# A fused two-layer kernel: 1/sqrt(v) from Ln and Exp, and token normalizations moved from VectorE to ScalarE

## The chip, the core and the metric

One Trainium2 chip, of which the kernel uses one core. The metric is the device time of one execution in microseconds; a kernel's time is the median of its runs. The engines are named as in the profile: PE (TensorE matmul), PEld (its weight loads), DVE (VectorE), ACT (ScalarE), POOL (GpSimd) and SP (the engine that issues most DMAs). They run side by side, each through its own instructions in a fixed order, and wait for each other by semaphores.

## What is computed

The input is a feature map of 4 images, 384 channels, 32 x 32 pixels (1024 tokens per image), all in float32. Two layers follow each other, each with a mixing part and a part on single tokens:

```python
x = x + _L0_conv_ref(_ln_c(x), ...)     # selective scan in 4 directions, layernorm, exact gelu
t = _to_tokens(x)
t = t + _L0_ffn_ref(_ln_t(t), ...)      # mixture of 4 experts, the best 2 per token, 384 -> 1536 -> 384
x = _from_tokens(t, x)
x = x + _L1_conv_ref(_ln_c(x), ...)     # attention, 8 heads of 64, queries = keys = values
t = _to_tokens(x)
t = t + _L1_ffn_ref(_ln_t(t), ...)      # two factorized layers with a gelu between
x = _from_tokens(t, x)
```

Every `_ln` subtracts the mean over the 384 channels of a token and divides by `sqrt(variance + eps)`. These square roots, and the subtract-and-scale behind some of them, are what the change touches. The scan's own step is `h = h * exp(dt * A) + dt * u * B`, with 16 states per channel.

## The kernel before

**The scan layer** (`scan_layer`, L192 on) goes through 32 units: 4 images, 4 directions, 2 halves of 512 positions. Each unit has 3 blocks of 128 channels, and each block 4 groups of states. In a group (`chunk`, L389 on) ACT computes `da` = Exp (L429) into one of two PSUM buffers, POOL multiplies `bx` (L420), DVE runs the recurrence over 512 positions (L434), DVE (L441) or POOL (L448) multiplies with C, and PE sums over states (L455). `project` (L293 on) prepares the next unit's `dt` meanwhile, with an Abs, Relu, Exp and Ln on ACT.

**The tail** of an image is the expert layer, the attention and the last token layer. It is written behind the scan of the next image, so that PE's work for one image lies beside the scan of the next; the last image's tail stands alone at the end. The steps that matter here:

- `spread` (L606, the router) transposes token tiles, takes their statistics on DVE (L633, L634), takes the root (L636, L637), scales the gate scores (L638), and in `places` (L666) works out with some fifty small DVE instructions which row of a gathered list each token goes to (`g_pos`, L778). It reloads the tokens (`xt`, L648), normalizes each tile of 128 tokens (128x384, L649, eight per image), and POOL scatters the tile's rows to two places each (L654).
- `experts` (L807) runs 11 slots of up to 256 gathered rows through one expert's two matrices. ACT does the Gelu (L888).
- `combine` (L904) loads the tokens (`xt`), gathers each token's two results into tiles `got` (POOL, L913; 128 x 2 x 384, tag `kw`), scales them on ACT (L920) and adds them on DVE (L924). It stores `xt` (L925).
- `prologue` (L930) takes statistics (`stats`, L516: L523, L524, then L525 and L526), normalizes in place in `xt` (`normalize`, L529: L531, eight per image), and PE transposes the tiles (L939) into `xc` for the attention. Writing in place, L531 has to wait until the store L925 has read `xt`.
- `last_layers` (L1049) uses `stats` as well; its `rstd` enters at L1102.

**The root** was taken in three steps: a Sqrt on ACT, a reciprocal on DVE, and a reload of the table set that has Exp and Ln, since Sqrt stands in another set. `exp_again` (L141) issues that reload just behind the Sqrt, with priority. A Gelu has the same pattern. In `layernorm` (L150), which normalizes over channels with PE's column sums, the root is L178 and the reciprocal L180, for each half of 512 positions: 4 halves per image, two before the scan and two behind it, 16 in all.

**The order of the work** isn't written by hand. A planner simulates the engines and orders each engine's instructions by that and by priorities; the router, `combine`, `prologue` and `last_layers` are pulled forward by a priority offset (`FORWARD`). A changed instruction can therefore move others, far from it, on all engines. Tiles rotate through a fixed number of buffers per tag (`kw` 8 or 10, `k12` 2 or 3, `k4` 5 or 4); a new tile waits until the one whose place it takes has been read for the last time.

`second_layer_exact` runs only when a sum in the attention grows past a limit, which doesn't happen with these inputs.

Of the kernel before, what the change touches and what calls it, by code (L numbers as in the profile page):

```python
# [11 lines left out]
AF = mybir.ActivationFunctionType  # L12
ALU = mybir.AluOpType
# [4 lines left out]
P = 128  # L18
B = 4
D = 384  # L20
# [28 lines left out]
MB = L // P  # L49
# [65 lines left out]
class Body:  # L115
# [25 lines left out]
    def exp_again(self, ins):  # L141

        with self.tc.issue_after(ins), self.tc.high_priority():
            self.nc.scalar.preload_act_table_set("natural_log_exp_and_others")

    def col(self, name, i):
        at = COL[name][0] + i
        return self.cols[:, at : at + 1]

    def layernorm(self, src, dst, eps, psum, work):  # L150

        nc = self.nc
        for i in range(NH):
            sl = halves(i)
            mean = psum.tile([P, HF], F32, tag="ps", name="ln_mean")
            for c in range(DC):
                nc.tensor.matmul(mean, self.ones, src[:, c, sl], start=(c == 0), stop=(c == DC - 1))
            for c in range(DC):
                nc.vector.scalar_tensor_tensor(
                    dst[:, c, sl], mean, -1.0 / D, src[:, c, sl], op0=ALU.mult, op1=ALU.add  # L160
                )

            sqs = []
            for c in range(DC):
                sq = work.tile([P, HF], F32, tag="k2", name="ln_sq", bufs=6)
                nc.scalar.activation(sq, dst[:, c, sl], AF.Square)
                sqs.append(sq)
            nm = HF // P
            var = psum.tile([P, HF], F32, tag="ps", name="ln_var")
            for m in range(nm):  # L170
                for c in range(DC):
                    nc.tensor.matmul(
                        var[:, m : m + 1], sqs[c][:, m * P : (m + 1) * P], self.ones[:, :1],
                        start=(c == 0), stop=(c == DC - 1),
                    )
            std = work.tile([P, nm], F32, tag="ln_std", name="ln_std", bufs=2)
            self.exp_again(
                nc.scalar.activation(std, var[:, :nm], AF.Sqrt, bias=eps, scale=1.0 / D).ins  # L178
            )
            nc.vector.reciprocal(std, std)  # L180
            rows = psum.tile([P, HF], F32, tag="ps", name="ln_rows")
            for m in range(nm):
                nc.tensor.matmul(
                    rows[:, m * P : (m + 1) * P], std[:, m : m + 1].to_broadcast([P, P]),
                    self.ident, start=True, stop=True,
                )
            for c in range(DC):
                nc.vector.tensor_mul(dst[:, c, sl], dst[:, c, sl], rows)
# [296 lines left out]
    def first_layer(self, b, room):  # L485

        self.experts(b, self.slots, room)
        with self.tc.high_priority(offset=FORWARD):
            xt = self.combine(b, *self.place, room)
            return self.prologue(xt, xt, room)  # L490

    def second_layer(self, b, xc, room, between):
        att = self.attention(xc, self.sums[:, b], room)
# [22 lines left out]
    def stats(self, xt, eps, room):  # L516

        nc = self.nc
        st = room.tile([P, MB, 6], "st", "st")
        mv = room.tile([P, MB, 2], "mv", "mv")  # L520
        rstd = room.tile([P, MB], "rstd", "rstd")
        for m in range(MB):
            nc.vector.bn_stats(st[:, m, :], xt[:, m, :])  # L523
            nc.vector.bn_aggr(mv[:, m, :], st[:, m, :])  # L524
        self.exp_again(nc.scalar.activation(rstd, mv[:, :, 1], AF.Sqrt, bias=eps).ins)  # L525
        nc.vector.reciprocal(rstd, rstd)  # L526
        return mv[:, :, 0], rstd

    def normalize(self, xt, mean, rstd, out):  # L529
        for m in range(MB):  # L530
            self.nc.vector.tensor_scalar(  # L531
                out[:, m, :], xt[:, m, :], mean[:, m : m + 1], rstd[:, m : m + 1],
                op0=ALU.subtract, op1=ALU.mult,
            )

# [68 lines left out]
    def spread(self, b, x1, room):  # L606


        nc = self.nc
        src = x1[b].rearrange("(c p) l -> p c l", p=P)  # L610
        st = room.tile([P, MB, 6], "r_st", "st")
        mv = room.tile([P, MB, 2], "r_mv", "mv")
        rstd = room.tile([P, MB], "r_rstd", "rstd")
        sc = room.tile([P, MB, NE], "sc", "sc")


        for m in range(0, MB, 2):
            x = room.tile([P, DC, 2 * P], "k4", "x")
            nc.sync.dma_start(out=x, in_=src[:, :, m * P : (m + 2) * P])
            xt = room.tile([P, 2, D], "k4", "xt")  # L620
            for o in range(2):
                ps = room.bank("p", "tt_ps")
                cols = slice(o * P, (o + 1) * P)
                for c in range(DC):
                    nc.tensor.transpose(ps[:, c * P : (c + 1) * P], x[:, c, cols], self.ident)
                for c in range(DC):
                    nc.tensor.matmul(
                        ps[:, D : D + NE], x[:, c, cols], self.wg[:, c, :],
                        start=(c == 0), stop=(c == DC - 1),
                    )  # L630
                nc.scalar.copy(xt[:, o, :], ps[:, :D])
                nc.vector.tensor_copy(sc[:, m + o, :], ps[:, D : D + NE])
                nc.vector.bn_stats(st[:, m + o, :], xt[:, o, :])  # L633
                nc.vector.bn_aggr(mv[:, m + o, :], st[:, m + o, :])  # L634
            nc.sync.dma_start(out=self.tokens(b)[:, m : m + 2, :], in_=xt)
        self.exp_again(nc.scalar.activation(rstd, mv[:, :, 1], AF.Sqrt, bias=self.eps5).ins)  # L636
        nc.vector.reciprocal(rstd, rstd)  # L637
        nc.vector.tensor_mul(sc, sc, rstd.unsqueeze(2).to_broadcast([P, MB, NE]))  # L638
        nc.vector.tensor_add(sc, sc, self.bg.unsqueeze(1).to_broadcast([P, MB, NE]))
        pos, gate, expert = self.places(sc, room)  # L640

        placed = []
        for m in range(MB):
            if m % 2 == 0:
                xt = room.tile([P, 2, D], "k4", "xt")
                nc.sync.dma_start(out=xt, in_=self.tokens(b)[:, m : m + 2, :])  # L648
            nc.vector.tensor_scalar(  # L649
                xt[:, m % 2, :], xt[:, m % 2, :], mv[:, m, :1], rstd[:, m : m + 1],  # L650
                op0=ALU.subtract, op1=ALU.mult,
            )
            for k in range(TOP):
                put = nc.gpsimd.indirect_dma_start(  # L654
                    out=self.rows[b][:, :],
                    out_offset=bass.IndirectOffsetOnAxis(ap=pos[:, k, m : m + 1], axis=0),
                    in_=xt[:, m % 2, :], in_offset=None,
                ).ins
                for other in placed:
                    self.tc.declare_no_dep(put, other, reason="rows of different tokens")  # L660
                for other in self.zeroed:
                    self.depend(put, other)
                placed.append(put)
        return (pos, gate), (expert, placed)
# [238 lines left out]

    def combine(self, b, pos, gate, room):  # L904

        nc = self.nc
        xt = room.tile([P, MB, D], "k12", "xt")
        nc.sync.dma_start(out=xt, in_=self.tokens(b))
        got = []
        for m in range(MB):  # L910
            got.append(room.tile([P, TOP, D], "kw", "got"))
            for k in range(TOP):
                nc.gpsimd.indirect_dma_start(  # L913
                    out=got[m][:, k, :], out_offset=None, in_=self.made[b][:, :],
# [8 lines left out]
            for k in range(TOP):  # L923
                nc.vector.tensor_add(xt[:, m, :], xt[:, m, :], ps[:, k, :D])  # L924
        nc.sync.dma_start(out=self.tokens(b), in_=xt)  # L925
        return xt

    def prologue(self, xt, xn, room):  # L930

        nc = self.nc
        mean, rstd = self.stats(xt, self.eps6, room)
        self.normalize(xt, mean, rstd, xn)
        xc = room.tile([P, DC, L], "k12", "xc")
        for c in range(DC):
            ps = room.two("tc_ps")
            for m in range(MB):
                nc.tensor.transpose(  # L939
                    ps[:, m // 4, m % 4 * P : (m % 4 + 1) * P], xn[:, m, c * P : (c + 1) * P],  # L940
                    self.ident,
                )
            nc.scalar.copy(xc[:, c, :], ps.rearrange("p o l -> p (o l)"))
        return xc
# [213 lines left out]
    def second_layer_exact(self):  # L1158

        nc, tc, a = self.nc, self.tc, self.a  # L1160
        with ExitStack() as ctx:
# [10 lines left out]
            for b in range(B):  # L1172
                xc = work.tile([P, DC, L], F32, tag="xc", name="xc", bufs=1)
                att = work.tile([P, HEADS // 2, L], F32, tag="att", name="att", bufs=1)
                with ExitStack() as part:
                    room = Room(tc, part, f"e{b}", EXACT)
                    room.open_banks(part, NARROW_BANKS)
                    xt = room.tile([P, MB, D], "k12", "xt")
                    nc.sync.dma_start(out=xt, in_=self.tokens(b))
                    nc.vector.tensor_copy(xc, self.prologue(xt, xt, room))  # L1180
                with ExitStack() as part:
                    psum = part.enter_context(tc.tile_pool(name=f"e{b}_a", bufs=2, space=PSUM))
                    self.attention_exact(xc, att, work, psum)
# [202 lines left out]
```

## Time and profile before

| | |
|---|---|
| time, median of 3 runs | 4483.56 us (4473.93 to 4485.39) |
| the profiled execution, its own time | 4517.48 us |
| its span, first to last instruction | 4513.6 us |
| mean granted TensorE clock | 0.831 |
| PE, DVE, ACT, POOL busy | 3440.6, 3010.8, 2534.3, 3037.0 us |
| ACT_TABLE_LOAD, all lines | 185 of 1283 ns each |
| - of these at the Sqrt lines L178, L525, L636 | 16 + 8 + 4 |
| - of these by `exp_again` (L144) | 92: 28 behind a Sqrt, 64 behind a Gelu |
| Sqrt | 263 ns (128x4), 301 ns (128x8) |
| reciprocals of the roots on DVE | 28, 171 to 192 ns in the mean |
| normalization of a tile, DVE, L649 and L531 | 64; median 474 and 472 ns, longest 2542 and 8690 ns |

How to read it: a line of the groups gives line, engine, operation, output and inputs, shape, count, then the busy time in us and the mean in ns of one, and after the second bar the engine's idle time just before these instructions with what ended it. A line of the time line gives the start and the length in us, engine, line and count of instructions that follow one another, and in brackets the idle time before. A line of the waits gives who waited for whom, the sum in us, how often, and the longest.

The scan stage ends near 3555 us. The first 650 us hold only the scan of the first image; from then on tail and scan lie side by side; from 3555 us to the end there is only the tail. The router's normalizations run at 849, 1883, 2983 and 3640 us, those of the prologue at 1444, 2574, 3608 and 4238 us.

### The profile page before, as it was taken

The page shows a single profiled execution, that of the slowest core. Times are in us where ns is not written, and L with a number is a line of the kernel's source. Part 1 is how long each engine was busy: PE and PEld are TensorE (multiplying, and loading weights), DVE is VectorE, ACT ScalarE, POOL GpSimd, SP SyncE. Part 2 cuts the span into 40 slices and gives each one's busy share as a digit, 9 for nine tenths or more (in the row PEclk, how much of TensorE's full clock was granted, in tenths as well). Part 3 has the DMA queues.
Part 4 walks back from the last instruction along what each step waited for, and adds up shares of the span by engine and source line. Part 5 has one row for each costly group of instructions (what it writes and reads, how often), then busy time and mean ns, then how long its engine had stood idle before and what let it go on. Part 6 is the DMA issues. An engine that isn't in the chain of part 4 may idle for free. (4 is left out here: it accounts for less than half of the span.)

```text
span 4513.6 us, 46925 instructions
## 1 busy us (share of the span) xinstructions
PE 3440.6 (76%) x13852; PEld 1652.0 (37%) x13852; DVE 3010.8 (67%) x4344; ACT 2534.3 (56%) x4406; POOL 3037.0 (67%) x1467
## 2 busy tenths in 40 slices
PE   6545554479894787669998588757998689999796
PEld 2111121145552222225555222214555445556333
DVE  4999997878878977977877777896778520002102
ACT  4555554456665676466666577556666444334554
POOL 4999998788987877778988778878889510000100
PEclk7666665589996898669998699858999789999897
DMA  4444554477886533457779443445787543344200
GB/s 119 118 123 118 146 136 106 137 230 209 231 240 181 149 84 104 130 159 226 210 220 275 137 114 101 115 139 170 232 244 232 169 157 115 107 127 153 75 16 15
DMA packets 404361, 684.81 MB, mean 152 GB/s; under 512 B 50944, under 2 KB 206464, under 8 KB 404096
## 3 DMA queue, kind: packets, MB, share of 16 engines
q1 hardware_dynamic: 395360, 656.16, 50.3%
q0 software_dynamic: 8192, 25.17, 1.7%
q8 instruction: 111, 1.82, 0.2%
q14 instruction: 154, 1.26, 0.1%
q10 hardware_dynamic: 544, 0.40, 0.0%
HBM read 561.47 MB, written 120.06 MB: 151 GB/s over the span
## 5 line engine op out<-in xcount | busy, mean ns | idle before, releaser
L420 POOL TENSOR_TENSOR bx<-dtr,bcs 128x1024 f32<-128x1024 f32 x768 | 1797.8, 2366 | 227.7 <-PE acc L455 103.5
L429 ACT ACTIVATE da<-dtr,nega 128x512 f32<-128x512 f32 x1536 | 1045.5, 691 | 1039.4 <-DVE bx L441 569.0
L448 POOL TENSOR_TENSOR bx<-bx,bcs 128x1024 f32<-128x1024 f32 x384 | 903.6, 2358 | 211.8 <-DVE bx L434 88.0
L455 PE MATMUL acc<-bx,sel 128*32 128x512 f32 x3072 | 511.8, 713 | 312.4 <-POOL bx L448 248.8
L879 PE MATMUL h_ps<-xc,w 128*128 128x256 f32 (+1 forms) x3168 | 680.1, 370 | 61.7 <-DVE xc L861 31.5
L895 PE MATMUL y_ps<-w,hs 128*128 128x384 f32 x1824 | 649.9, 509 | 49.8 <-ACT hs L888 44.1
L879 PEld LDWEIGHTS h_ps<-xc,w 128*128 128x128 f32 x3168 | 557.2, 200 | 253.4 <-issue 120.4
L434 DVE TENSOR_TENSOR_SCAN bx<-da,carry,bx 128x512 f32<-128x512 f32 x384 | 474.0, 1269 | 118.6 <-POOL bx L420 65.5
L434 DVE TENSOR_TENSOR_SCAN bx<-da,bx 128x512 f32<-128x512 f32 x384 | 452.2, 1209 | 129.2 <-POOL bx L420 70.3
L434 DVE TENSOR_TENSOR_SCAN da<-da,carry,bx 128x512 f32<-128x512 f32 x384 | 476.5, 1273 | 67.9 <-ACT da L429 62.6
L441 DVE TENSOR_TENSOR bx<-da,bcs 128x512 f32<-128x512 f32 x768 | 509.8, 679 | 3.8
L434 DVE TENSOR_TENSOR_SCAN da<-da,bx 128x512 f32<-128x512 f32 x384 | 456.3, 1218 | 60.7 <-ACT da L429 44.2
L895 PEld LDWEIGHTS y_ps<-w,hs 128*128 128x128 f32 x1824 | 352.3, 198 | 341.7 <-issue 86.4
L992 ACT ACTIVATE ex<-s_ps 128x512 f32<-128x512 f32 x512 | 299.4, 591 | 274.9 <-PE s_ps L987 259.9
L987 PE MATMUL s_ps<-w 64*128 64x512 f32 x1024 | 308.4, 674 | 83.1 <-ACT ex L992 74.2
L1077 POOL TENSOR_TENSOR xt<-xt,wb 128x3072 f32<-128x3072 f32 x4 | 26.8, 6708 | 477.5 <-DMA w<-in_w 345.5
L1036 PE MATMUL o_acc<-ex,vt 128*64 128x512 f32 x1024 | 295.6, 658 | 0.8 <-ACT att L1044 0.8
L455 PEld LDWEIGHTS acc<-bx,sel 128*32 128x32 f32 x3072 | 77.7, 117 | 596.0 <-POOL bx L448 363.8
L884 ACT ACTIVATE hs<-h_ps,bb 128x256 f32<-128x256 f32 (+1 forms) x528 | 194.0, 447 | 128.8 <-PE h_ps L879 128.5
L899 DVE TENSOR_TENSOR y<-y_ps,bb 128x384 f32<-128x384 f32 x76 | 41.6, 548 | 237.6 <-PE y_ps L895 237.6
L913 POOL DMA_INDIRECT got<-made,g_pos x64 | 60.8, 950 | 192.4 <-PE f_acc L1136 159.1
L987 PEld LDWEIGHTS s_ps<-w 64*128 64x128 f32 x1024 | 81.1, 192 | 266.8 <-ACT ex L992 149.1
(216 smaller groups left out, 4021.9 us busy)
## 6 DMA issues: line engine op xcount, KB each, us to landing
w<-in_w SPq DMA_DIRECT2D x352, 576.0 KB
dtr<-dd SPq DMA_DIRECT2D x1536, 128.0 KB
bcs<-rows SPq DMA_DIRECT2D x512, 128.0 KB
dd<-one_e SPq DMA_DIRECT2D x96, 256.0 KB
dd<-mag SPq DMA_DIRECT2D x96, 256.0 KB
rows<-zero SPq DMA_DIRECT2D x76, 192.0 KB
xs<-rows SPq DMA_DIRECT2D x32, 384.0 KB
made<-y SPq DMA_DIRECT2D x32, 384.0 KB
```

The source lines that it names most:

```text
L420: pool = nc.gpsimd.tensor_mul(bx, dtr[q][1], bc[:, 0].unsqueeze(1).to_broadcast([P, 2, HF])).ins
L429: nc.scalar.activation(da, dtr[q][0][:, j, :], AF.Exp, scale=nega[:, col : col + 1])
L434: nc.vector.tensor_tensor_scan(run(h), run(da), run(bx[:, j, :]), 0.0 if first else hold, ALU.mult, ALU.add,)
L441: dve = nc.vector.tensor_mul(bx[:, j, :], h, cg).ins
L448: pool = nc.gpsimd.tensor_mul(bx, bx, cg.unsqueeze(1).to_broadcast([P, 2, HF])).ins
L455: nc.tensor.matmul(acc[lo : lo + DB, :], sel, out[q][:, j, :], start=(g == 0), stop=(g == NG - 1),)
L879: nc.tensor.matmul(ps[:, r, :], w1[(f + r) // wf][:, c, (f + r) % wf * P : ((f + r) % wf + 1) * P], xc[:, c, :], start=(c == 0), stop=(c = ...
L884: nc.scalar.activation(hs[:, f + r, :], ps[:, r, :], AF.Identity, bias=bb[:, f + r : f + r + 1])
L895: nc.tensor.matmul(out[:, :D], hs[:, f, t * P : (t + 1) * P], w2[f // wf][:, f % wf, :], start=(f == 0), stop=(f == FC - 1),)
L987: nc.tensor.matmul(ps[:, o, :], w[rows, j * P : (j + 1) * P], w[rows, halves(i)], start=True, stop=True,)
L992: ins = nc.scalar.activation(ex[:, o, :], ps[:, o, :], AF.Exp, scale=HD**-0.5, accum_out=sums[:, t, 2 * j + o, i : i + 1],).ins
L1036: ins = nc.tensor.matmul(out[cols, :], made[t][1][:, j, cols], ex[:, o, :], start=(j == 0), stop=(j == MB - 1),).ins
```

## The change

The root becomes two instructions of ACT, `Ln(scale * v + eps)` and `Exp(-0.5 * that)`, both of the set that the scan uses, so that the Sqrt, its table load, the reload and the reciprocal all go. A normalization `(x - mean) * rstd` becomes an ACT Identity with a scale `rstd` and a bias `less = -mean * rstd`, which a new DVE instruction makes once per image and site (128x8). In the prologue its output is no longer `xt` itself but the first half of the tile `got` of the same tokens, which `combine` now returns as well.

```diff
+    def inverse_root(self, out, var, eps, scale=1.0):
+
+        self.nc.scalar.activation(out, var, AF.Ln, bias=eps, scale=scale)
+        self.nc.scalar.activation(out, out, AF.Exp, scale=-0.5)
...
             std = work.tile([P, nm], F32, tag="ln_std", name="ln_std", bufs=2)
-            self.exp_again(
-                nc.scalar.activation(std, var[:, :nm], AF.Sqrt, bias=eps, scale=1.0 / D).ins
-            )
-            nc.vector.reciprocal(std, std)
+            self.inverse_root(std, var[:, :nm], eps, scale=1.0 / D)
...
-            xt = self.combine(b, *self.place, room)
-            return self.prologue(xt, xt, room)
+            xt, xn = self.combine(b, *self.place, room)
+            return self.prologue(xt, xn, room)
...
-        self.exp_again(nc.scalar.activation(rstd, mv[:, :, 1], AF.Sqrt, bias=eps).ins)
-        nc.vector.reciprocal(rstd, rstd)
+        self.inverse_root(rstd, mv[:, :, 1], eps)
         return mv[:, :, 0], rstd
 
-    def normalize(self, xt, mean, rstd, out):
-        for m in range(MB):
-            self.nc.vector.tensor_scalar(
-                out[:, m, :], xt[:, m, :], mean[:, m : m + 1], rstd[:, m : m + 1],
-                op0=ALU.subtract, op1=ALU.mult,
-            )
+    def less_mean(self, mean, rstd, room, tag):
+
+        less = room.tile([P, MB], tag, "less")
+        self.nc.vector.scalar_tensor_tensor(less, mean, -1.0, rstd, op0=ALU.mult, op1=ALU.mult)
+        return less
...
-        self.exp_again(nc.scalar.activation(rstd, mv[:, :, 1], AF.Sqrt, bias=self.eps5).ins)
-        nc.vector.reciprocal(rstd, rstd)
+        self.inverse_root(rstd, mv[:, :, 1], self.eps5)
         nc.vector.tensor_mul(sc, sc, rstd.unsqueeze(2).to_broadcast([P, MB, NE]))
         nc.vector.tensor_add(sc, sc, self.bg.unsqueeze(1).to_broadcast([P, MB, NE]))
+        less = self.less_mean(mv[:, :, 0], rstd, room, "r_less")
         pos, gate, expert = self.places(sc, room)
...
-            nc.vector.tensor_scalar(
-                xt[:, m % 2, :], xt[:, m % 2, :], mv[:, m, :1], rstd[:, m : m + 1],
-                op0=ALU.subtract, op1=ALU.mult,
-            )
+            nc.scalar.activation(
+                xt[:, m % 2, :], xt[:, m % 2, :], AF.Identity,
+                bias=less[:, m : m + 1], scale=rstd[:, m : m + 1],
+            )
...
-        return xt
+        return xt, [got[m][:, 0, :] for m in range(MB)]
...
         mean, rstd = self.stats(xt, self.eps6, room)
-        self.normalize(xt, mean, rstd, xn)
+        less = self.less_mean(mean, rstd, room, "less")
+        for m in range(MB):
+            nc.scalar.activation(
+                xn[m], xt[:, m, :], AF.Identity, bias=less[:, m : m + 1], scale=rstd[:, m : m + 1]
+            )
```

The transposes of the prologue read `xn[m]` in place of `xn[:, m, ...]`. The path that isn't taken with these inputs passes the parts of `xt` as `xn`, so there the normalization stays in place.

More of the change, by code (lines that the diff above doesn't have):

```diff
@@ L939, in prologue @@
                 nc.tensor.transpose(
-                    ps[:, m // 4, m % 4 * P : (m % 4 + 1) * P], xn[:, m, c * P : (c + 1) * P],
+                    ps[:, m // 4, m % 4 * P : (m % 4 + 1) * P], xn[m][:, c * P : (c + 1) * P],
                     self.ident,
@@ L1179, in second_layer_exact @@
                     nc.sync.dma_start(out=xt, in_=self.tokens(b))
-                    nc.vector.tensor_copy(xc, self.prologue(xt, xt, room))
+                    xn = [xt[:, m, :] for m in range(MB)]
+                    nc.vector.tensor_copy(xc, self.prologue(xt, xn, room))
                 with ExitStack() as part:
```

## Prediction

> **What bounds the kernel now.** I read the shares of busy time first, then two stages side by side, then the waits, and last the time line around the instructions that the change touches. Shares alone mislead here: no engine is over 76%. The answer by stretches (columns: busy us and instructions of PE, PEld, DVE, ACT, POOL, then granted clock, DMA share, GB/s) parts the scan stage, which ends near 3555 us, from the tail:
>
> ```profile
> 0.00:3555.00 3555.00, 2605.36 (x10366) 1218.45 (x10367) 2870.61 (x4013) 2113.56 (x3542) 2970.44 (x1411) 0.81 0.58 166
> 3555.00:4513.60 958.60, 835.23 (x3487) 433.55 (x3487) 140.17 (x331) 420.76 (x864) 66.54 (x56) 0.90 0.31 100
> 3700.00:4200.00 500.00, 480.93 (x1993) 283.21 (x1992) 48.54 (x85) 195.01 (x389) 14.69 (x10) 0.98 0.38 120
> ```
>
> In the scan stage POOL is busy 2970 of 3555 us (84%) and DVE 2871 (81%): the two hand `bx` to each other, and both bind. ACT, 59%, feeds them. The tail belongs to PE, most of all 3700 to 4200 (481 of 500).
>
> The waits say what ACT does with its free time. "ACT da" is the Exp that feeds the scan through two PSUM buffers:
>
> ```profile
> ACT da L429 <- DVE bx L441: 569.0, 343, 9.7
> ACT da L429 <- DVE bx L434: 348.5, 372, 16.5
> ```
>
> ACT waits over 900 us for DVE, so work moved from DVE to ACT goes from a bound engine to one with room. The groups by line give what is moved and removed:
>
> ```profile
> L178 ACT ACT_TABLE_LOAD x16 | 20.5, 1283 | 4.8 <-PE ln_var L172 4.6
> L525 ACT ACT_TABLE_LOAD x8 | 10.3, 1283 | 0.1
> L636 ACT ACT_TABLE_LOAD x4 | 5.1, 1283 | 0.1
> L649 DVE TENSOR_SCALAR xt<-xt,mv,rstd 128x384 f32<-128x384 f32 x32 | 30.4, 1009 | 2.3 <-DMA xt<-x 2.3
> L531 DVE TENSOR_SCALAR xt<-xt,mv,rstd 128x384 f32<-128x384 f32 x32 | 23.0, 791 | 7.9 <-DMA x<-xt 7.9
> ```
>
> The means of L649 and L531 (1009, 791 ns) stand far above their medians (474, 472 ns). The time line of the first prologue shows why:
>
> ```profile
> 1440.48 6.93 POOL L420 TENSOR_TENSOR bx<-dtr,bcs 128x1024 f32<-128x1024 f32 x3
> 1443.54 11.41 DVE L531 TENSOR_SCALAR xt<-xt,mv,rstd 128x384 f32<-128x384 f32 x8
> 1447.38 2.33 POOL L448 TENSOR_TENSOR bx<-bx,bcs 128x1024 f32<-128x1024 f32 x1
> 1449.68 2.33 POOL L420 TENSOR_TENSOR bx<-dtr,bcs 128x1024 f32<-128x1024 f32 x1
> 1458.40 2.35 POOL L448 TENSOR_TENSOR bx<-bx,bcs 128x1024 f32<-128x1024 f32 x1 [6.39 <-DVE bx L434]
> ```
>
> Eight normalizations of 0.47 us take 11.41 us; the first lasts 8.69 us and ends as POOL falls idle at 1452. POOL then idles 6.39 us for want of DVE's scans. Such a DVE instruction stands still while POOL works.
>
> **Part 1: no Sqrt.** 28 Sqrt (16 layernorm halves, 8 in stats, 4 in the router) lose their load and the reload behind them: 56 x 1.283 = 71.8 us of ACT, 42 of them (53.9 us) in the scan stage. Ln replaces Sqrt at its 0.26 to 0.30 us; an Exp is added, about 0.23 us by the Exp L678 (128x32). 28 DVE reciprocals go (2.7 + 1.5 + 0.7 = 4.9 us). What of it lies on the path? A block on ACT starves the scan when it outlasts the buffers:
>
> ```profile
> 672.88 1.28 ACT L178 ACT_TABLE_LOAD   x1
> 674.17 0.26 ACT L178 ACTIVATE ln_std<-ln_var,eps 128x4 f32<-128x4 f32 x1
> 674.45 1.28 ACT L144 ACT_TABLE_LOAD   x1
> 675.75 1.30 ACT L429 ACTIVATE da<-dtr,nega 128x512 f32<-128x512 f32 x2
> 676.54 2.47 DVE L434 TENSOR_TENSOR_SCAN da<-da,carry,bx 128x512 f32<-128x512 f32 x2 [1.66 <-ACT da L429]
> ```
>
> A block of 2.85 us gave DVE 1.66 us of idle time; a Gelu with its loads (1144.79 to 1150.15, 5.36 us) gave 4.45. So DVE loses the block less about 1 us. The new block, 0.5 us, costs nothing. But of 21 sites in the scan stage I find only two with that idle time (1.23 and 1.66): 3 us. The rest is the chain of a layernorm. In seven halves the Sqrt starts the moment its load ends, so up to 7 x 1.28 = 9 us; in six the reciprocal queues behind scans on DVE (0.3 to 1.4 us, 4.5 in all), where the Exp follows Ln on ACT. I take half of this 13.5, since PE and DVE often wait for PE's own sums there: 3 + 7 = **10 us**. Bounds: 0 (ACT's room hides it all) and 21 x 1.66 + 13.5 = 48. The Trainium skill ("ScalarE: Activation LUTs", Rules for kernel authors) budgets about 2.7 us per switch of set; 56 would be 151 us of ACT. Every row here has 1283 ns, and the sum goes by that.
>
> **Part 2: normalizations by ACT, in the scan stage** (routes 0 to 2 and prologues 0 and 1; 40 of the 64 instructions). DVE gives up 27.0 us (24 of L649) and 16.6 us (16 of L531): 43.6 us, waits included. It gets a new instruction per site, `less` (128x8, both inputs in SBUF). The router's small products of that kind, L638, L639 and L763, last 0.16 to 0.19 us alone and 2.32 to 2.34 us when POOL is busy, one POOL instruction; 8.69 us is the worst seen at L531. I take 2.33 x 5 = 11.7 us; bounds 0.16 and 8.69 each. The same skill's page "SBUF — State Buffer" (Who interferes with whom) speaks against a full gain here: a DVE instruction with two SBUF inputs contends with a POOL instruction that reads SBUF, as does a tensor_scalar in a two-port mode, while ACT never waits. By that rule alone `less` keeps a wait for the one POOL instruction under way, at most 5 x 2.35 = 11.7 us, and part 2 gives no less than 15; the 8.69 us of L531 goes beyond it, so the trace's worst stays a bound.
>
> On ACT a 128x384 Identity with scale and bias from SBUF isn't in the trace. Nearest: L920, same size, one such operand, 584 ns; L362, 128x512 with one, 719 ns. I take 0.65 us, bounds 0.58 and 0.72. Eight in a row are 5.2 us, so DVE idles about 5.2 - 1 = 4.2 us. At four of the five sites the old ones stood in a row; the planner may place the new ones so: 4 x 4.2 = 17 us. What remains is 43.6 - 11.7 - 17 = **15 us**. Bounds: 43.6 - 0.8 = 43 when the eight are spread between the `da`, and 43.6 - 43.5 - 21 = -21 when each `less` waits the worst time and all five go in a row.
>
> **Part 3: the tail.** The in-place normalization had to wait until the store of `xt` had read it; the new one writes the gathered rows:
>
> ```profile
> 3608.03 3.21 DVE L531 TENSOR_SCALAR xt<-xt,mv,rstd 128x384 f32<-128x384 f32 x8 [5.50 <-DMA x<-xt]
> ```
>
> Prologue 2 ended at 3611.24. New: statistics done at 3601.96, then 0.30 + 0.23 + 0.2 + 8 x 0.65 = 5.9, so 3607.9: 3.3 us earlier; late next is ACT. Prologue 3: 4241.63 against 4234.24 + 5.9 + 0.58 for an output copy between: 0.9 us. Route 3: from L638 (3640.09) to L679 (3646.14) DVE spends 6.05 us, with eight normalizations and a wait of 2.30 us for the reloaded `xt` in between; without them the chain is some 1.2 us, 4.9 less before the scatters, which wait for `g_pos`. Sum 9.1; I take **7**, as PE's 481 of 500 us behind it doesn't shrink; bounds 0 and 9.1. The last layers of batch 3 gain nothing: rstd isn't used before L1102, 5 us later. The gathered tiles are held longer, until PE has transposed them; the next user of that tag, attention's `w`, needs `xc` and so those transposes anyway: 0.
>
> **Sum.** 10 + 15 + 7 = 32 us. The profiled execution took 4517.48 us (span 4513.6, 3.9 outside it), 33.9 above the median; I take the 32 off the median, 4483.56: **4452 us**.
>
> **Rivals.** *Full gain* (4414): the Identities fall between the `da` and the stalls were worth more: 20 + 43 + 7 = 70. For it: ACT's room; against: normalizations stood in rows. *Nothing to be had* (4476): POOL, busier than DVE, is the true bound, so DVE's relief turns into more waiting for `bx` from POOL (135.7 us already), and only the 7 of the tail stay. Against it: POOL's idle gaps behind these sites (11.3, 6.4, 4.3 us) are waits for DVE. *Slower* (4514): the first Identity holds ACT's in-order queue while `less`, or the reloaded row, is late; every `da` behind it, and then the scan, waits. The trace has such a hold: the router's Exp L678 stood 14.10 us for DVE. Five sites at 14.1 + 4.2 are 91.5 us, less 43.6 + 10 + 7: +31. It decides from a hold H with 5 x (H + 4.2) = 60.6, H = 7.9 us. Against it: while `less` waits for POOL, DVE couldn't have scanned either. That the loads come back, if the compiler takes another set for Ln, would cost part 1 alone and lie near 4462.
>
> **How the numbers follow.** Forecast (gain 15 to 55) 0.50, full gain 0.16, nothing 0.17, slower 0.17. The planner rewrites the order of all engines for any edit; no row prices that, and it is why the forecast has no more. This kernel's measurement tells apart about 0.3%, 13.5 us: faster 0.66, same 0.17, slower 0.17. The range takes in the first three cases with the bounds of part 2: from 4402 (82 gained: part 1 at 30, part 2 at 43, part 3 at 9) to 4490 (6 lost: part 2 at -20, the others at 10 and 4).
>
> **What would show it.** Right: table loads fall from 185 to 129, none at the Ln lines; DVE's busy time falls by about 55 us, ACT's by about 23 (71.8 - 6.4 for the Exp - 41.6 for 64 Identities); POOL's gaps behind routes and prologues shrink; the prologue at 3602 starts its transposes without a wait for the store. Wrong: "DVE bx/da <- ACT da" grows, ACT idles long before an Identity for `less`, `less` lasts over 5 us, or a wait "DVE <- POOL bx" grows by what DVE gave up.

## The result, and the profile after

The changed kernel takes 4554.6 us (median of 4 runs, 4544.23 to 4562.8), the kernel before, on the same chip, 4478.75 us (4472.73 to 4485.39). The ratio is **1.0168, interval 1.0139 to 1.0197**: slower by about 76 us, where 4452 us had been predicted. The profiled execution took 4558.59 us, 4 us above its median, with a span of 4556.7 us and a mean granted clock of 0.833 (before 0.831), so the clock isn't the reason. (The profile before is of an execution of 4517.48 us. The two profiles lie 41 us apart, not 76: they show where time goes, and the price is taken from the medians.)

First the groups of the profile after, the table loads (but for nine at L230, L353, L208 and L998) and what is new on DVE and ACT:

```profile
L144 ACT ACT_TABLE_LOAD x64 | 82.1, 1283 | 1.1
L888 ACT ACT_TABLE_LOAD x44 | 56.5, 1283 | 0.8
L355 ACT ACT_TABLE_LOAD x27 | 34.6, 1283 | 4.3 <-DMA dd<-one_e 3.3 <-PE dt_ps L360 0.5
L431 ACT ACT_TABLE_LOAD x25 | 32.1, 1283 | 0.4
L533 DVE SCALAR_TENSOR_TENSOR less<-mv,rstd 128x8 f32<-128x8 f32 x8 | 30.5, 3816 | 0.6 <-ACT rstd L149 0.6
L1134 ACT ACT_TABLE_LOAD x16 | 20.5, 1283 | 0.3
L649 ACT ACTIVATE xt<-xt,less,rstd 128x384 f32<-128x384 f32 x32 | 19.8, 696 | 6.1 <-DVE carry L447 3.9 <-DVE less L533 1.1 <-DMA xt<-x 1.1
L938 ACT ACTIVATE got<-xt,less,rstd 128x384 f32<-128x384 f32 x32 | 19.6, 694 | 25.5 <-DVE less L533 25.5
L148 ACT ACT_TABLE_LOAD x6 | 7.7, 1283 | 4.1 <-PE ln_var L177 4.1
L149 ACT ACT_TABLE_LOAD x6 | 7.7, 1283 | 0.1
```

(Lines of the scan stand 2 further down than before: L355 is the Ln in `project`, L431 the Exp `da`, L436 the recurrence, L148 and L149 the new Ln and Exp.) The loads at the Sqrt lines are gone, and so are the 28 reloads behind them: L144 fell from 92 to 64. But two lines that had none before, L355 and L431, now have 52, and the new pair has 12. With the nine not shown there are 197 loads, where there were 185 and 129 had been predicted.

The time line shows what a pair of them does, in the first image's scan (start, length, engine, line):

```profile
467.09 0.62 ACT L354 ACTIVATE one_e<-mag 128x512 f32<-128x512 f32 x1
467.73 1.28 ACT L355 ACT_TABLE_LOAD   x1
469.02 0.63 ACT L355 ACTIVATE lnw<-one_e 128x512 f32<-128x512 f32 x1
469.68 0.63 ACT L357 ACTIVATE one_e<-one_e 128x512 f32<-128x512 f32 x1
470.33 1.28 ACT L431 ACT_TABLE_LOAD   x1
471.62 1.30 ACT L431 ACTIVATE da<-dtr,nega 128x512 f32<-128x512 f32 x2
472.42 2.34 DVE L436 TENSOR_TENSOR_SCAN bx<-da,bx 128x512 f32<-128x512 f32 x2 [2.63 <-ACT da L431]
```

Before, the same step of ACT had no load in it:

```profile
435.13 0.63 ACT L352 ACTIVATE one_e<-mag 128x512 f32<-128x512 f32 x1
435.88 0.63 ACT L353 ACTIVATE lnw<-one_e 128x512 f32<-128x512 f32 x1
436.54 0.63 ACT L355 ACTIVATE one_e<-one_e 128x512 f32<-128x512 f32 x1
437.44 1.35 ACT L429 ACTIVATE da<-dtr,nega 128x512 f32<-128x512 f32 x2 [0.27 <-DVE bx L441]
```

Ln has a load ahead of it, the next Exp has another, and so on, about once per channel block: each time a set is put in that lacks the other function. From the start of the Identity ahead of Ln (`one_e`) to the point where the next `da` can start, ACT took 2.04 us before (435.13 to 437.17) and takes 4.53 now (467.09 to 471.62); the two `da` buffers don't cover that, and DVE stands idle for 2.63 us. The windows 120 to 600 us, ahead of all changed normalizations, give the sum (columns: busy us and instructions of PE, PEld, DVE, ACT, POOL, then granted clock, DMA share, GB/s). First before, then after:

```profile
120.00:600.00 480.00, 255.10 (x759) 60.19 (x762) 441.56 (x578) 252.10 (x394) 474.74 (x207) 0.67 0.51 129
```

```profile
120.00:600.00 480.00, 248.71 (x708) 59.18 (x708) 412.65 (x538) 281.19 (x406) 444.45 (x194) 0.67 0.41 117
```

ACT gained 29 us of work, and DVE and POOL each lost 29 to 30: nearly all of what ACT does more is taken from the scan, although ACT is idle 40% of this stretch. The waits of the same window name it, before and then after:

```profile
DVE bx L434 <- ACT da L429: 9.8, 44, 1.2
```

```profile
DVE bx L436 <- ACT da L431: 37.7, 48, 2.7
```

The DVE instruction that writes the `y` of the 21st channel block starts at 660.2 us before and at 715.6 after; that of the 96th and last block at 3554 and 3662 us. The extra loads end at 851.27 us, where the first `exp_again`, behind a Gelu, puts in the set with both functions. From there on no Ln and no Exp of the scan has one.

The rest of what the prediction looked at, stage by stage and then ACT's waits for DVE, in the profile after:

```profile
0.00:3662.00 3662.00, 2632.40 (x10410) 1223.96 (x10410) 2879.08 (x3990) 2195.14 (x3662) 2986.19 (x1427) 0.81 0.54 163
3662.00:4556.70 894.70, 803.16 (x3444) 414.23 (x3443) 116.67 (x271) 401.57 (x848) 51.41 (x40) 0.93 0.30 99
```

```profile
ACT da L431 <- DVE bx L443: 643.7, 357, 14.4
ACT da L431 <- DVE bx L436: 302.6, 379, 17.9
```

The scan stage is 107 us longer and the tail 64 us shorter: besides the slower scan, the planner's new order puts work of the tail beside it. ACT still waits 946 us for DVE in these two rows, 917.5 before, so it has as much free time as the prediction saw.

Three of the four prologues wait for `less`. The first one:

```profile
1467.56 0.30 ACT L148 ACTIVATE rstd<-mv,eps 128x8 f32<-128x8 f32 x1 [1.01 <-DVE mv L526]
1467.89 0.21 ACT L149 ACTIVATE rstd<-rstd 128x8 f32<-128x8 f32 x1
1469.20 8.69 DVE L533 SCALAR_TENSOR_TENSOR less<-mv,rstd 128x8 f32<-128x8 f32 x1
1469.72 1.25 POOL L378 TENSOR_TENSOR lnw<-lnw,mag 128x512 f32<-128x512 f32 x1
1470.94 4.62 POOL L422 TENSOR_TENSOR bx<-dtr,bcs 128x1024 f32<-128x1024 f32 x2
1475.53 2.33 POOL L450 TENSOR_TENSOR bx<-bx,bcs 128x1024 f32<-128x1024 f32 x1
1477.92 4.89 ACT L938 ACTIVATE got<-xt,less,rstd 128x384 f32<-128x384 f32 x8 [7.91 <-DVE less L533]
```

`less`, 0.15 us by itself, lasts until POOL's run of four more instructions is over (1477.86), as the first normalization did before. In a run below it is a third of that, so what it costs was put to the test.

### The profile page after: what moved, and what is told of

The parts are those of the page before. It is cut to its first block, busy times and chain, and to the rows that moved or that the text cites. A ratio compares the mean times of both kernels' runs of the same rounds, so it can differ in the third digit from the quotient of the medians.

```text
span 4556.7 us, 46939 instructions
## 1 busy us (share of the span) xinstructions
PE 3435.6 (75%) x13852; PEld 1638.2 (36%) x13852; DVE 2995.8 (66%) x4260; ACT 2596.7 (57%) x4510; POOL 3037.6 (67%) x1467
## 5 line engine op out<-in xcount | busy, mean ns | idle before, releaser
L431 ACT ACTIVATE da<-dtr,nega 128x512 f32<-128x512 f32 x1536 | 1046.3, 691 | 1030.5 <-DVE bx L443 643.7
L879 PE MATMUL h_ps<-xc,w 128*128 128x256 f32 (+1 forms) x3168 | 670.6, 367 | 45.1 <-DVE xc L861 23.4
L895 PE MATMUL y_ps<-w,hs 128*128 128x384 f32 x1824 | 640.1, 504 | 41.3 <-ACT hs L888 38.5
L436 DVE TENSOR_TENSOR_SCAN bx<-da,bx 128x512 f32<-128x512 f32 x384 | 454.2, 1211 | 176.6 <-POOL bx L422 95.8
L436 DVE TENSOR_TENSOR_SCAN bx<-da,carry,bx 128x512 f32<-128x512 f32 x384 | 474.3, 1270 | 141.3 <-ACT da L431 70.5
L436 DVE TENSOR_TENSOR_SCAN da<-da,carry,bx 128x512 f32<-128x512 f32 x384 | 478.3, 1275 | 81.3 <-ACT da L431 66.8
L436 DVE TENSOR_TENSOR_SCAN da<-da,bx 128x512 f32<-128x512 f32 x384 | 456.1, 1218 | 46.7 <-ACT da L431 31.1
L998 ACT ACTIVATE ex<-s_ps 128x512 f32<-128x512 f32 x512 | 299.3, 590 | 205.6 <-PE s_ps L993 205.3
L347 PE MATMUL dt_ps<-xd,wdt 12*128 12x512 f32 x192 | 129.2, 758 | 65.7 <-ACT mag L386 38.5
```

The source lines that it names most:

```text
L431: nc.scalar.activation(da, dtr[q][0][:, j, :], AF.Exp, scale=nega[:, col : col + 1])
L436: nc.vector.tensor_tensor_scan(run(h), run(da), run(bx[:, j, :]), 0.0 if first else hold, ALU.mult, ALU.add,)
L879: nc.tensor.matmul(ps[:, r, :], w1[(f + r) // wf][:, c, (f + r) % wf * P : ((f + r) % wf + 1) * P], xc[:, c, :], start=(c == 0), stop=(c = ...
L895: nc.tensor.matmul(out[:, :D], hs[:, f, t * P : (t + 1) * P], w2[f // wf][:, f % wf, :], start=(f == 0), stop=(f == FC - 1),)
L998: ins = nc.scalar.activation(ex[:, o, :], ps[:, o, :], AF.Exp, scale=HD**-0.5, accum_out=sums[:, t, 2 * j + o, i : i + 1],).ins
```

## The experiments

All ratios are to the kernel before on the same chip (medians 4515.34 us for runs 1 to 4, 4515.12 for 5 to 8 and 4514.19 for 9 to 12). "Root" is Ln and Exp in place of Sqrt, reload and reciprocal; "norm" is the normalizations by ACT. The first question was which half lost the time, and whether by the loads.

**1. The change with the set put in place.** One line into the changed kernel, ahead of its first Exp:

```diff
+            nc.scalar.preload_act_table_set("natural_log_exp_and_others")
```

> The change, plus one preload of the table set that holds Ln and Exp, ahead of the scan's first Exp. Theory A (table loads came back: the old reload behind the first Sqrt had put that set in place at 21 us; without it the scan of the first image alternates between two sets, 66 loads of 1.283 us up to 851 us, some 53 us of delay by block 23 of the scan): about 130 loads in all and a time near 4555 - 53 = 4502 us or less. Theory B (the loss lies in the normalizations on ScalarE, held by the new DVE instruction, three of which last 8.7 to 10.2 us): loads fall, but the time stays within 15 us of 4555.

Measured: 4517.76 us, ratio 1.0008 (0.9997 to 1.0019). The loss is gone, and with it every load at Ln and Exp:

```profile
L144 ACT ACT_TABLE_LOAD x64 | 82.1, 1283 | 1.1
L889 ACT ACT_TABLE_LOAD x44 | 56.5, 1283 | 0.8
L1135 ACT ACT_TABLE_LOAD x16 | 20.5, 1283 | 0.3
L231 ACT ACT_TABLE_LOAD x5 | 6.4, 1283 | 0.1
L208 ACT ACT_TABLE_LOAD x1 | 1.3, 1283 | 1.7 <-PEq L1385 1.7
L999 ACT ACT_TABLE_LOAD x1 | 1.3, 1283 | 0.0
```

The order of the instructions on every engine is that of the changed kernel, so the quotient, 1.0168 / 1.0008 = 1.016 (±0.003, the two intervals added in squares), is a price of the loads alone. It divides ratios from two chips, on which the kernel before takes 4478.75 and 4515.34 us, and holds only as far as both kernels differ by that much there; the changed kernel's own median is 37 us (0.8%) above run 1's. The prices from one chip, in runs 2, 3 and 5, are firmer.

**2. The root alone, with the set in place, and 3. without it.** The kernel before, with `inverse_root` in the three places, its normalizations on DVE (the last line of the diff stands in run 2 alone):

```diff
-            self.exp_again(
-                nc.scalar.activation(std, var[:, :nm], AF.Sqrt, bias=eps, scale=1.0 / D).ins
-            )
-            nc.vector.reciprocal(std, std)
+            self.inverse_root(std, var[:, :nm], eps, scale=1.0 / D)
...
+            nc.scalar.preload_act_table_set("natural_log_exp_and_others")
```

> The kernel before with the root as Ln and Exp and the same preload; the normalizations stay on DVE. Theory A: part 1 of the forecast alone, about 10 us under the kernel before (4479): 4469, at most 48 under it. Theory B says nothing against that. If the time is above 4490, the root itself costs, or the planner's new order does.

> The kernel before with the root as Ln and Exp, without any preload; normalizations on DVE. Theory A: about 195 loads, the first image late by some 53 us, time near 4469 + 53 = 4522 us. Theory B: within 15 us of the kernel before, near 4470.

Measured: 4537.77 us, 1.0052 (1.0035 to 1.0069), with 129 loads, and 4594.76 us, 1.0174 (1.0157 to 1.0191), with 195. The order is the same in both, so the 66 loads cost 1.0174 / 1.0052 = 1.012 (±0.002), 57 us. The surprise is run 2: with all 56 loads and 28 reciprocals gone and nothing come back, it is slower than before.

**4. Norm alone.** Before's Sqrt, reload and reciprocal; `less_mean` and the Identities as in the change (shown for the router; the prologue's are those of the change).

```diff
+        less = self.less_mean(mv[:, :, 0], rstd, room, "r_less")
...
-            nc.vector.tensor_scalar(
-                xt[:, m % 2, :], xt[:, m % 2, :], mv[:, m, :1], rstd[:, m : m + 1],
-                op0=ALU.subtract, op1=ALU.mult,
+            nc.scalar.activation(
+                xt[:, m % 2, :], xt[:, m % 2, :], AF.Identity,
+                bias=less[:, m : m + 1], scale=rstd[:, m : m + 1],
```

> The kernel before with the normalizations on ScalarE and the root still by Sqrt with its reload. Theory A: no loads come back, so the time is not above the kernel before by more than 10 us (forecast of parts 2 and 3: 4479 - 22 = 4457). Theory B: slower than before by most of the 76 us lost: 4530 or more.

Measured: 4491.57 us, **0.9947 (0.9932 to 0.9963)**, faster than both kernels. `less` was much cheaper here:

```profile
L532 DVE SCALAR_TENSOR_TENSOR less<-mv,rstd 128x8 f32<-128x8 f32 x8 | 9.9, 1243 | 0.1
```

**5. The loads by themselves, in the kernel before.** Nothing of the change; only the reload behind the Sqrt of `layernorm` is left out for the first two images, so that the set with both functions isn't put in place. The order on all engines stays before's, but for one pair of neighbouring PE instructions at 2744 us.

```diff
-            self.exp_again(
-                nc.scalar.activation(std, var[:, :nm], AF.Sqrt, bias=eps, scale=1.0 / D).ins
-            )
+            root = nc.scalar.activation(std, var[:, :nm], AF.Sqrt, bias=eps, scale=1.0 / D).ins
+            if again:
+                self.exp_again(root)
...
-                self.layernorm(x, x, self.eps6, psum, work)
+                self.layernorm(x, x, self.eps6, psum, work, again=b > 1)
```

> Before's Sqrt, reciprocals and order, but the preload behind the Sqrt is left out in layernorm for the first two images, so that the set with both Ln and Exp isn't put in place ahead of the first image's scan. Nothing else is changed, and the planner's order is before's. Theory (the loads between Ln and Exp in the first image's scan are what the changed kernel lost): some 60 more loads than before's 185, all ahead of 900 us, and a ratio of 1.012 to 1.016 against before, the 57 to 72 us that the pairs of runs so far gave. Rival (the loads are covered, since ScalarE isn't the engine that bounds, and the loss came from the planner's order): the loads show, and the ratio stays below 1.004.

Measured: 4572.3 us, 1.0122 (1.0103 to 1.0142), 57 us more. This is the cleanest price: 237 loads instead of 185, with those of the scan's Ln and Exp back.

```profile
L353 ACT ACT_TABLE_LOAD x27 | 34.6, 1283 | 1.0 <-PE dt_ps L358 0.3 <-DMA dd<-mag 0.2
L429 ACT ACT_TABLE_LOAD x27 | 34.6, 1283 | 0.5
```

One stretch, from the first channel block's `y` to the 21st's, holds the same instructions of PE, DVE and POOL in both kernels, 553 us before and 592 here; before, then this run:

```profile
107.00:660.00 553.00, 300.08 (x910) 77.63 (x909) 507.91 (x685) 296.21 (x461) 547.74 (x238) 0.67 0.51 131
```

```profile
114.00:706.00 592.00, 307.12 (x910) 79.85 (x910) 508.81 (x685) 346.31 (x499) 550.51 (x238) 0.67 0.48 123
```

ACT has 38 instructions more, the loads (48.8 of its 50.1 us), and the stretch is 39 us longer: a load costs 1.03 us of its 1.28, 80%. The rival, that ACT's idle time covers them, falls.

**6. `less` by ACT, in the change with the preload, and 7. in norm alone.**

```diff
-        self.nc.vector.scalar_tensor_tensor(less, mean, -1.0, rstd, op0=ALU.mult, op1=ALU.mult)
+        neg = room.tile([P, MB], tag + "_n", "neg")
+        self.nc.scalar.mul(neg, rstd, -1.0)
+        for m in range(MB):
+            self.nc.scalar.activation(
+                less[:, m : m + 1], mean[:, m : m + 1], AF.Copy, scale=neg[:, m : m + 1]
+            )
```

> The changed kernel with the preload ahead of the first Exp, and `less` made by ScalarE itself (one small instruction for -rstd and eight small ones, mean times -rstd) instead of by one VectorE instruction. Theory A (the first Identity's wait of 8 to 9 us for the late `less` lies on the path of each of three prologues): 25 us less than with `less` on VectorE, a ratio near 0.995 against before. Theory B (the wait is covered by the rest of the stage, and the 20 us that root and normalizations together lost against the normalizations alone lie elsewhere): a ratio of 0.999 to 1.003, as with `less` on VectorE (1.0008).

> Before's Sqrt, reload and reciprocal, the normalizations by ScalarE, and `less` by ScalarE. `less` took 9.9 us in all in the run with it on VectorE, 3.3 at most. Theory A (a late `less` costs its length): a ratio of 0.993, some 5 us below the normalizations alone (0.9947). Theory B (nothing waits for it at the end): 0.993 to 0.997, not to be told from 0.9947. Either way below both kernels.

Measured: 4501.4 us, 0.9970 (0.9956 to 0.9984), and 4493.52 us, 0.9957 (0.9941 to 0.9973). Run 6 lies 0.4% below run 1, between the two theories (A had 25 us, 17 were found), and run 7 isn't told apart from run 4. But `less` by ACT also brings another order, from the second image on, and the runs below show that another order alone can move the time by nearly as much.

The question still open was why the root without any extra load lost 0.5%. Theory I: its instructions have a price (the Exp stands behind Ln in ACT's queue, where the reciprocal was on DVE). Theory O: the planner's new order has it.

**8. The root with DVE's reciprocal kept.** Exp with +0.5 and then the reciprocal: all the work of run 2 and 28 DVE instructions more.

```diff
-        self.nc.scalar.activation(out, out, AF.Exp, scale=-0.5)
+        self.nc.scalar.activation(out, out, AF.Exp, scale=0.5)
+        self.nc.vector.reciprocal(out, out)
```

> Before's normalizations, the root as Ln, then Exp with scale +0.5 and VectorE's reciprocal behind it, with the preload at the start: all of the work of the run with the root alone (ratio 1.0052), and 36 reciprocals of VectorE more. The planner gives it another order. Theory O (the root's loss of 0.5% is the planner's order, not the price of the instructions): the ratio has no reason to lie at or over 1.0052; anything within 0.995 to 1.012 fits, and one below 1.003 speaks for it. Theory I (the Exp as a second ScalarE instruction in the chain from variance to rows costs it, behind what is queued on ScalarE): a ratio of 1.005 or more, since the Exp is still there and the reciprocal comes on top.

(Of the reciprocals 28 run, not 36 as expected.) Measured: 4542.4 us, 1.0062 (1.0044 to 1.0080). Inconclusive: it fits I, and O doesn't forbid it.

**9. and 10. Another order for nothing, before and with the root.** One line in the router, four instructions in a whole execution, that multiplies by one:

```diff
         nc.vector.reciprocal(rstd, rstd)
+        nc.vector.tensor_scalar_mul(rstd, rstd, 1.0)
         nc.vector.tensor_mul(sc, sc, rstd.unsqueeze(2).to_broadcast([P, MB, NE]))
```

> Before, with one VectorE instruction more per image in the router (rstd times 1.0, 128x8, four in all, under 1 us of work together), which changes nothing in the values but makes the planner write another order from the second image on. Theory O (the planner's order by itself moves the time by several tenths of a per cent, and the root's +0.5% is such a move): a ratio that leaves 0.999 to 1.001, on either side, by up to 0.6%. Theory I (order hardly matters, the root's instructions have a price): within 0.998 to 1.002.

> The root with the preload and before's normalizations (ratio 1.0052 so far), with the same four VectorE instructions in the router. Theory I: 1.004 to 1.007 again, and 1.005 times what the same four instructions make of before. Theory O: the 0.5% doesn't come back as such; the ratio to before with the four instructions leaves 1.003 to 1.007, and may fall to 0.998.

Measured: before with the line 4529.54 us, **1.0029** (1.0017 to 1.0041); the root with it 4517.86 us, **1.0010** (0.9999 to 1.0021). Four instructions of 0.17 us each when alone (2.4 and 4.8 us together, waits for POOL included) moved the kernel before by 15 us, +0.3%, and run 2 by -0.4%, and with the line in both the root is 0.998 of its counterpart (±0.002), where it was 1.0052. A price of the root's instructions would have stayed: theory I falls, and the order is what is left.

**11. The root in `layernorm` alone, and 12. in `stats` and router alone**, each with the preload.

> The root by Ln and Exp in layernorm alone, with the preload at the start; router and prologue keep Sqrt, reload and reciprocal, and the normalizations stay on VectorE. Theory I with the price in layernorm's chain (the rows' waits grew there, VectorE waited 22.5 us for them in one stretch of 240 us where it was 5.9): 1.005. Theory I with the price in router and prologue: 1.000. Theory O: no link with the part changed, 0.996 to 1.010, and this ratio times that of the other half need not make 1.0052.

> The other half: the root by Ln and Exp in router and prologue alone, layernorm keeps Sqrt, reload and reciprocal, normalizations on VectorE. Theory I: this ratio times that of the root in layernorm alone makes 1.0052 within 0.2%. Theory O: it doesn't, by more than 0.2%, or one of the two is over 1.0052 by itself.

Measured: 4572.64 us, 1.0123 (1.0108 to 1.0138), and 4511.18 us, 0.9992 (0.9983 to 1.0002). The product is 1.0115, not 1.0052, and the half of a change costs more than twice the whole. Run 11 has 153 loads, 32 fewer than before, none of them at Ln or `da`. Against run 2 it has 24 loads more (31 us of ACT), but leaving out the same 24 gained only 0.1% in run 12. Its scan keeps before's pace through most of two images (the 42nd block starts 0.4 us later, at 1470 us) and falls behind in the third, by 38 us at the 57th block and 73 at the 69th. Theory I can't give such a sum. What is left is the order, which would then move this kernel by up to 1.2%, as much as the loads do; that size is argued, for no run changes the order alone by so much. Shown by itself is the 0.3% of run 9.

## Why the prediction was wrong, point by point

**The step that failed** is the last sentence of the rivals: "That the loads come back, if the compiler takes another set for Ln, would cost part 1 alone and lie near 4462." They did come back, and cost 1.2% on one chip (runs 5, and 3 against 2: 57 us) and 1.6% by the change against run 1 (72 us), not the 10 us of part 1. Two things were wrong in it. It asked only whether the loads at the *changed* lines return, one for one. But the reload behind the second Sqrt had put in place the set that serves `project`'s Ln and the scan's Exp, and it stayed until the next Sqrt at 651.71 us: it was part of what the scan needed. In the profile before:

```profile
29.61 1.28 ACT L178 ACT_TABLE_LOAD   x1
32.08 0.26 ACT L178 ACTIVATE ln_std<-ln_var,eps 128x4 f32<-128x4 f32 x1 [1.18 <-PE ln_var L172]
32.36 1.28 ACT L144 ACT_TABLE_LOAD   x1
```

Run 5, which leaves this reload out (and the three others ahead of the first two images' scans), shows it. And the sentence took the price from part 1, where the loads sit in layernorms, mostly beside other waits. These sit between two `da`, where the scan has two buffers of slack, and 80% of each is lost.

The loads aren't the whole miss. Between the ratio forecast (0.993) and the one measured (1.017) lie 2.4%, of which 1.2 to 1.6% are theirs. Run 1, without them, still stands at 1.0008: the gain of 0.7% didn't come. The parts below say how much of it can be placed.

The trace of before held the clue: no load at L353 or L429, though the first load of the kernel, for the Exp in L206, doesn't tell whether its set has Ln. The question "who put this set in place?" leads to L144. The Trainium skill ("ScalarE: Activation LUTs", Table sets: the hidden batching unit) says that Ln then Exp need one load, since one set has both; that is true of run 1 but not of the change, where a set without the other function was taken each time. The skill's page "ScalarE activation tables: per-element evaluation and per-set limits" (Table sets in the compiler and the runtime) has the back end place loads per block by the greedy longest run. If the first scan counts as one block, that would be one load for it, as in run 1; the rows of after show 64 at L355, L431, L148 and L149 up to 851 us. The measurement decides: which set is taken isn't to be relied on.

**Part 1, +10 us.** The sites were read rightly: run 2 has the 129 loads and run 1 131, and ACT's busy time falls in run 1 from 2534.3 to 2511.8 us, 22.5 less where 23 had been forecast. The gain in time didn't show: with the root and no extra loads the kernel went by +0.5% (run 2), +0.6% (run 1 against 4), +0.1% (run 6 against 7) and -0.2% (run 10 against 9), in four orders. 10 us is 0.2%, less than these four differ among themselves, so whether part 1 gains anything can't be told.

**Part 2, +15, and part 3, +7.** Norm alone gave -0.53%, 24 us, against 22 forecast; run 1 against run 2 gives -0.4%, run 7 -0.4%, and only the change against run 3, both with the loads, shows none (0.9994 ±0.003). The size fits; the place can't be read. In run 4 the scan's last recurrence ends at 3536 us (before 3547), but the last block's `y`, which waits for PE's sum, starts at 3559 (before 3554): by the one mark 11 us are gained in the scan stage, by the other none. And run 9 moved 15 us, over half of this, for nothing. So the hit is in part luck: that ACT does the normalizations cheaper is supported by three pairs of four, not shown apart from the order.

Of its terms, the Identity was 0.69 us alone and eight in 4.89 us (estimate 0.65 and 5.2): right. `less` was mis-sized: 11.7 us for five; in the change two prologues took 8.69 and 8.70 us and route 0 2.35, 20 in all. Its wait is for the whole run of POOL, which the sum had kept as a bound only. For the third prologue, from its root at 3627.09 to the end of the Identities at 3643.22 are 16.1 us where part 3 had 5.9, because `less` lasted 10.16; for the fourth, alone in the tail, 5.7: right. Route 3 from L637 to L679 takes 4.3 us where 1.2 had been forecast (6.05 before): the Exp L678 stood behind six Identities in ACT's queue. DVE's busy time fell by 15 us, not 55 (the sum's own 11.7 us for `less` would have left 46): of the 58 us of normalizations and reciprocals 30.5 came back as `less`, and 13 in other DVE instructions that grew longer (`z` at the old L1102 from 11.3 to 16.8 us).

**The rivals.** "Slower" named a hold of 7.9 us of the first Identity as the point from which it decides, and the three prologues have 7.91, 7.99 and 9.37. Yet with those same holds run 1 is at 1.0008, and with `less` on ACT at 0.9970: by itself this mechanism makes no loss against before. The sign was right and its reason was not: luck. That no row prices the planner's order was said in the prediction. Its size, 0.3% in run 9 and 0.4% between runs 2 and 10, is about half of all that had been summed up (0.7%), and a chance of 0.66 for "faster" took no account of that.

## What to carry to other kernels

Before an instruction that switches tables is removed, list which later functions live on the set that it leaves behind, and put that set in place by hand at the start; then look at the loads by line, at the unchanged lines too. Price a hold on a feeding engine by the buffers behind it, not by that engine's share of idle time. And where a planner writes the order, run a change that does nothing beside the real one: what such a line moves (here 0.3%) is the least that a sum of small terms has to beat. The best version found is the normalizations by ACT with the old root, 0.9947 of before; the root is only to be had with the preload, and no pair of runs here shows a clear gain from it.

## What the runs showed of the hardware

A table load takes 1283 ns in every row, and where the instruction behind it waits for nothing else, it starts 0.01 us later; no second cost of a switch shows on ACT. What a load costs the kernel depends on the place: 1.03 us each between two `da` (run 5). Ln and Exp of 128x4 take 262 and 205 ns, of 128x8 300 and 208. A DVE instruction of 0.15 us (`less`) with two inputs in SBUF lasted 8.69 to 10.16 us, through four and more POOL instructions that followed each other closely, not for one; the Trainium skill ("SBUF — State Buffer", Who interferes with whom) tells of the exclusive lock for one instruction, and these rows go beyond it.
